# Where the variance of a batch norm is summed in a sparse graph-attention kernel: after the first attention, or beside it

## The chip, the cores and the metric

The kernel runs on one core of one Trainium2 chip, as one launch. The metric is the device time of that launch in microseconds, the median of a few runs. The core has five engines with an instruction queue each: TensorE (PE in the profile, with PEld for its weight loads), VectorE (DVE), ScalarE (ACT), GpSimd (POOL) and SyncE (SP, which here only issues DMAs). Each queue is worked off in order.

## The reference, cut to what matters

Four graph layers on 3327 nodes with 512 features each (8 heads of 64), over one sparse adjacency matrix. Each layer normalises its input, applies a layer function and adds the result to the input. Layer 0 is an attention followed by a batch norm over the nodes; layer 1 averages the neighbours' rows (GraphSAGE); layers 2 and 3 are attentions.

```
# layer 0, after the layer norm h of x
attn    = softmax(where(adj > 0, leaky_relu(s_dst[i] + s_src[j], 0.2), -9e15))
h_prime = einsum('ijh,jhd->ihd', attn, Wh).reshape(n, 512)
mean    = jnp.mean(h_prime, axis=0)
var     = jnp.var(h_prime, axis=0)
h_prime = gamma * (h_prime - mean) * jax.lax.rsqrt(var + 1e-5) + beta
x       = x + relu(h_prime)
# layer 1 starts from the layer norm of this x
```

Mean and variance run over all 3327 nodes, for each of the 512 features. So nothing of layer 1 can start before the last node of layer 0 is done.

## The kernel before, in words

The nodes are padded to 3328 and taken in 26 blocks of 128 (`NB`); a block is two groups of 64 destination nodes (`GB`). For each of the 52 groups, lists built at the start of the kernel hold the source nodes that the group needs, in chunks of 128; the chunk counts fall from 22 for the first group to 5 and 4 for the last (`CAPS`), 359 in all. A unit is up to three chunks of one group (`UNIT`), and there are 135 units.

The function `sparse` runs the layers one after the other. In `attend(layer, ...)` (from L1170) the loop over units does the following. `load(i + 1)` issues from POOL's queue one gather for each chunk of the next unit (L1165, an indirect DMA of 128 table rows into `rows`, which has six buffers); in layer 0 DVE also takes the mask bits out of the rows (`on`, L1252) and ACT turns them into `mask` (L1258). For the unit itself DVE makes `mx` (L1266, a maximum of two broadcasts, written to PSUM) and `wgt` (L1273, times the mask; three buffers), and PE multiplies `wgt` with the gathered rows into `facc` (L1287), where the last column of each head is the softmax's denominator. Between DVE's work and PE's matmuls of a unit, `later()` is called once. It lets every group that is through take one step of its `ending`: ACT copies the sums (L1215), DVE takes the reciprocal (L1219), ACT scales the eight heads into the result (L1225), and a finished block is reported. Then `later()` calls `tick()`.

In layer 0 the result goes to `y` (`bn_y`), which holds all 26 blocks in SBUF, a reported block is appended to `whole`, and `tick` advances a generator, `beside` (from L1339). That generator puts other work into the attention, one small step for each unit: 50 steps for the products of layer 1's weights (`fb_ps`, `fwx_ps`), then one step for each block of `y`, a matmul with a matrix of ones (L1374) that adds up the 128 nodes of the block in PSUM (`bmean_ps`). Every partition of the result holds the same sums. A float32 matmul appears as two in the profile.

PE, DVE and ACT are scheduled by hand inside `attend`: their instructions stay in the order in which the Python code issues them. The order in POOL's and SP's queues is left to the framework's scheduler.

After the attention come the mean (L1376), then the variance stage (pool `fbn`, L1398 to L1407): 13 rounds over two blocks each, in which DVE subtracts the mean into `bn_d` (two buffers), ACT squares it in place and PE adds the squares up in `var_ps`. The reciprocal root (`rsqrt`, L708 to L719) and the scaling of `gam`, `mean` and `bet` follow. Then `normed(c)` scales two blocks at a time, adds x, takes the layer norm for layer 1 and writes it to `h_dram`, while `own(c)` multiplies finished blocks with layer 1's weights. Layer 1 gathers its neighbours from `h_dram` (`z_rows`), so it starts when all 26 blocks have been written.

Of the kernel before, what the change touches and what calls it, by code (L numbers as in the profile page):

```python
# [23 lines left out]
F32 = mybir.dt.float32  # L24
# [7 lines left out]
AF = mybir.ActivationFunctionType  # L32
ALU = mybir.AluOpType
# [5 lines left out]
P = 128  # L39
H = 8  # L40
F = 64
D = H * F
# [8 lines left out]
GB = 64  # L51
CAPS = (22, 15, 13, 12, 11, 10, 9, 9, 9) + 4 * (8,) + 6 * (7,) + 11 * (6,) + 21 * (5,) + (4,)
HALF = 64
BATCH = 4
WB = 16
LNB = 5
ROW = H * (F + 1) + H
UNIT = 3
# [482 lines left out]
def constants(ctx, tc, N):  # L541
# [18 lines left out]

    c["pow"] = pw = const.tile([P, WB], F32, name="fpow")
    pi = const.tile([P, WB], I32, name="fpow_i")
    nc.gpsimd.iota(pi, pattern=[[-1, WB]], base=0, channel_multiplier=1)
    nc.vector.tensor_single_scalar(pi, pi, WB - 1, ALU.bitwise_and)
    for k in range(WB):
        nc.vector.memset(pw[:, k : k + 1], float(1 << k))
    nc.vector.scalar_tensor_tensor(pw, pi, 0.0, pw, ALU.is_equal, ALU.mult)
    c["bit"] = bit = const.tile([P, WB], U16, name="fbit")
    for k in range(WB):
# [4 lines left out]
class Projection:  # L574
# [13 lines left out]
    def stats(self, q):  # L588

        nc, pp, k = self.tc.nc, self.pool, q % LNB  # L590
        if q >= self.NB:
            return
        if k == 0:
            mv = pp.tile([P, LNB, nc.vector.BN_AGGR_DIM], F32, name="ln_mv", tag="ln_mv", bufs=2)
            self.mv, self.xs = mv, []
        xt = pp.tile([P, D], F32, name="ln_x", tag="ln_x", bufs=LNB + 4)
        nc.sync.dma_start(xt, self.xin[q * P : (q + 1) * P, :])
# [3 lines left out]
        self.xs.append(xt)  # L601
        if k == LNB - 1 or q == self.NB - 1:
            n = k + 1
# [4 lines left out]
    def norms(self):  # L608
        nc = self.tc.nc
        if self.step is not None:  # L610
            c0, n, mv, xs, step = self.step
            self.step = None
            r = step()
            ng = self.pool.tile([P, LNB, 1], F32, name="ln_ng", tag="ln_ng", bufs=2)
            if c0 + n == self.NB:
# [5 lines left out]
    def begin(self):  # L621
        self.step, self.have, self.turns, self.hT, self.wh, self.row, self.r = None, {}, 0, {}, {}, {}, {}
        for q in range(LNB):
            self.stats(q)
# [77 lines left out]
def rsqrt(nc, pool, cs, v, scale=1.0, bufs=3):  # L702


    n = v.shape[1]
    y = pool.tile([P, n], F32, name="rs_y", tag=f"rs_y{n}", bufs=bufs)
    g = pool.tile([P, n], F32, name="rs_g", tag=f"rs_g{n}", bufs=bufs)
    nc.scalar.activation(g, v, AF.Ln, scale=scale, bias=cs["eps"])  # L708
    nc.scalar.activation(y, g, AF.Exp, scale=-0.5)

    def step():
        h = pool.tile([P, n], F32, name="rs_h", tag=f"rs_h{n}", bufs=bufs)
        nc.vector.tensor_scalar(h, v, -0.5 * scale, -0.5 * EPS, ALU.mult, ALU.add)
        if n == 1:
            nc.vector.tensor_scalar(g, y, y, h, ALU.mult, ALU.mult)
        else:
            nc.vector.tensor_tensor(g, y, y, ALU.mult)
            nc.vector.tensor_tensor(g, g, h, ALU.mult)
        nc.vector.scalar_tensor_tensor(y, g, 1.5, y, ALU.add, ALU.mult)  # L719
        return y  # L720

    return step
# [17 lines left out]
class Following:  # L740
# [34 lines left out]
    mean = Projection.mean  # L775
# [361 lines left out]
def sparse(ctx: ExitStack, tc: tile.TileContext, t: dict, out: bass.AP, WA, ls, cs, idx, rdeg, first):  # L1137
# [5 lines left out]
    nc = tc.nc  # L1143
    N = out.shape[0]
    NP = t["x"].shape[0]
    NB = NP // P
# [3 lines left out]
    def used(c):  # L1150
        return min(P, N - c * P)
# [6 lines left out]
    ones = cs["ones"]  # L1158
# [171 lines left out]
    with ExitStack() as mx:  # L1330
        mid = mx.enter_context(tc.tile_pool(name="fmid", bufs=1))

        y = mid.tile([P, NB, D], F32, name="bn_y")
# [3 lines left out]
        whole = []  # L1337

        def beside(wp, wps):  # L1339

            nc.sync.dma_start(bias, t["L1_gnn_b_comb"].partition_broadcast(P))
            nc.sync.dma_start(gam, t["L0_gnn_gamma"].partition_broadcast(P))
            nc.sync.dma_start(bet, t["L0_gnn_beta"].partition_broadcast(P))
            for k, (wn, bn) in enumerate((("L1_WsT", "L1_gnn_b_self"), ("L1_WnT", "L1_gnn_b_nb"))):
                Wc = wp.tile([P, KC, D], F32, name="fWc", tag="fWc", bufs=1)
                nc.sync.dma_start(Wc, t["L1_gnn_W_comb"][k * D : (k + 1) * D, :].rearrange("(kc p) o -> p kc o", p=P))
                bcol = wp.tile([P, KC, 1], F32, name="b_col", tag="b_col", bufs=1)
                with nc.allow_non_contiguous_dma(reason="512 biases, once"):
                    nc.sync.dma_start(bcol[:, :, 0], t[bn].rearrange("(kc p) -> p kc", p=P))
                yield  # L1350
                b_bc = wp.tile([P, KC, P], F32, name="b_bc", tag="b_bc", bufs=1)
                nc.scalar.copy(b_bc, bcol.to_broadcast([P, KC, P]))
                ps = wps.tile([P, D], F32, name="fb_ps", tag="beside", bufs=1)
                for kc in range(KC):
                    nc.tensor.matmul(ps, b_bc[:, kc, :], Wc[:, kc, :], start=(kc == 0), stop=(kc == KC - 1))
                    yield
                nc.vector.tensor_tensor(bias, bias, ps, ALU.add)
                for fc in range(KC):
                    WT = wp.tile([P, KC, P], F32, name="fWT", tag="fWT", bufs=2)
                    nc.sync.dma_start(WT, t[wn][:, fc * P : (fc + 1) * P].rearrange("(kc p) o -> p kc o", p=P))  # L1360
                    yield
                    ps = wps.tile([P, D], F32, name="fwx_ps", tag="beside", bufs=1)
                    for kc in range(KC):
                        nc.tensor.matmul(ps, WT[:, kc, :], Wc[:, kc, :], start=(kc == 0), stop=(kc == KC - 1))
                        yield
                    w = wp.tile([P, D], F32, name="fwx", tag="fwx", bufs=1)
                    nc.scalar.copy(w, ps)
                    nc.sync.dma_start(wx_dram[k, fc, :, :], w)
            mean_ps = wps.tile([P, D], F32, name="bmean_ps", tag="beside", bufs=1)
            for c in range(NB):  # L1370
                while len(whole) <= c:
                    yield
                k = used(c)
                nc.tensor.matmul(mean_ps, ones[:k, :], y[:k, c, :], start=(c == 0), stop=(c == NB - 1))  # L1374
                yield
            nc.vector.tensor_scalar_mul(mean, mean_ps, 1.0 / N)  # L1376

        mean = mid.tile([P, D], F32, name="bn_mean")
        with tc.tile_pool(name="beside", bufs=1) as wp, tc.tile_pool(name="beside_ps", bufs=1, space=PSUM) as wps:
            bg = beside(wp, wps)  # L1380

            def done(c, hp, pool):
                yield
                whole.append(c)
                yield

            attend(0, *first, done, lambda: next(bg, None), y)
            for _ in bg:
                pass
# [5 lines left out]
        gps = mx.enter_context(tc.tile_pool(name="fsage_ps", bufs=2, space=PSUM))  # L1395
        two = [P, 2, D]
        with tc.tile_pool(name="fbn", bufs=1) as bp:
            var_ps = gps.tile([P, D], F32, name="var_ps", tag="n_ps")  # L1398
            for c in range(0, NB, 2):
                d = bp.tile(two, F32, name="bn_d", tag="bn_d", bufs=2)  # L1400
                nc.vector.tensor_tensor(d, y[:, c : c + 2, :], mean.unsqueeze(1).to_broadcast(two), ALU.subtract)
                nc.scalar.activation(d, d, AF.Square)
                for i in range(2):
                    k = used(c + i)
                    nc.tensor.matmul(var_ps, ones[:k, :], d[:k, i, :], start=(c + i == 0), stop=(c + i == NB - 1))
            var = bp.tile([P, D], F32, name="bn_var")
            nc.scalar.mul(var, var_ps, 1.0 / N)  # L1407
            nc.vector.tensor_tensor(gam, gam, rsqrt(nc, bp, cs, var, bufs=1)(), ALU.mult)
            nc.vector.tensor_tensor(mean, mean, gam, ALU.mult)
            nc.vector.tensor_tensor(bet, bet, mean, ALU.subtract)  # L1410
# [78 lines left out]
        for b in range(NB):  # L1489
            ps = list(zip_longest(*(list(ls.batches(b * PG + u, SUNIT)) for u in range(PG))))  # L1490
# [132 lines left out]
```

## Time and profile before

| what | us |
|---|---|
| median of 3 runs | 2559.43 (2559.01 to 2560.68) |
| the profiled execution | 2553.76 |
| its span | 2551.8 |

Where the span goes, and how busy the engines are in it, in us:

| stretch | stage | PE | DVE | ACT | POOL |
|---|---|---|---|---|---|
| 0 to 319 | adjacency, lists, projections of layer 0 | 204.7 | 215.2 | 134.5 | 19.0 |
| 319 to 807 | first attention | 328.2 | 452.8 | 175.1 | 341.3 |
| 807 to 842 | variance | 28.1 | 16.8 | 15.5 | 0.0 |
| 842 to 940 | batch norm, layer norm, own products | 77.1 | 82.8 | 36.9 | 7.6 |
| 940 to 1447 | layer 1, neighbours | 457.6 | 141.6 | 208.2 | 333.2 |
| 1447 to 2049 | second attention | 445.4 | 482.0 | 340.0 | 344.5 |
| 2049 to 2551 | third attention | 283.9 | 461.2 | 158.2 | 341.9 |

A line of the profile names the source line, the engine, the operation, what it writes and reads, and then either the start and duration (timeline) or the count, the busy time and the mean in ns (groups). In brackets or behind a bar stands how long the engine was idle just before, and what ended that idle time. A name after "<-" there is the releaser that the profile infers; "issue" means that it shows nothing that was waited for. Issuing an instruction is not counted as busy, so a queue can be full at less than full busy time.

### The profile page before, as it was taken

The numbers are of one execution on the slowest core, as the hardware profiler recorded it, in microseconds if no ns is written. First come the engines' busy times: TensorE is split into PE (matmuls) and PEld (weight loads), VectorE is DVE, ScalarE is ACT, GpSimd is POOL, SyncE is SP. The second block draws the span as 40 slices with busy tenths as digits, with TensorE's granted clock in tenths as the row PEclk, the third lists the DMA queues.
The fourth block names the chain that finished last, engine by engine and source line by source line (L and its number), as shares of the span: only waits on it lengthen the run. The fifth ranks groups of instructions, "written<-read, shape, count | busy, mean of one in ns | idle before, by whom it ended". The sixth has DMA issues, their size and how long they took to land.

```text
span 2551.8 us, 53690 instructions
## 1 busy us (share of the span) xinstructions
PE 1825.0 (72%) x21112; PEld 1161.8 (46%) x21112; DVE 1852.3 (73%) x2272; ACT 1068.3 (42%) x3810; POOL 1387.4 (54%) x1482
## 2 busy tenths in 40 slices
PE   3667756776677698889999657778878646566653
PEld 2444444454454342223333356656555435555543
DVE  7667579999997850222333499999877279999996
ACT  4553212333445332334455214667766601233444
POOL 1000176777772026777777277776554067777672
PEclk9767889988888899999999778897877787777787
DMA  8773198888783566788888478887665178888784
GB/s 326 288 263 123 43 296 276 280 281 260 241 253 95 191 217 198 234 247 260 254 267 255 125 223 242 235 240 232 199 200 177 39 215 232 236 238 243 232 238 123
DMA packets 189057, 562.57 MB, mean 220 GB/s; under 512 B 37764, under 2 KB 42304, under 8 KB 185470
## 3 DMA queue, kind: packets, MB, share of 16 engines
q0 software_dynamic: 115456, 404.86, 53.3%
q1 hardware_dynamic: 73342, 154.20, 17.0%
q8 instruction: 169, 2.77, 0.4%
q14 instruction: 90, 0.74, 0.1%
HBM read 499.26 MB, written 59.68 MB: 219 GB/s over the span
## 4 chain that ended last, share of the span: by engine, by line
PE 30%; DVE 24%; issue 13%; ACT 9%; DMA 8%; POOL 3%; DVEq 0%; SPq 0%; POOLq 0%; ACTq 0%
DVE mx L1266 12%; PE facc L1287 8%; DVE wgt L1273 8%; PE sage_acc L1522 4%; DMA z_rows<-h_dram,idx 4%; PE p_wh L866 4%; DMA rows<-table,idx 3%; PE n_ps L1471 3%; PE p_wh L808 3%; ACT fhp L1225 2%; POOL z_rows L1165 2%; PE s_ps L1445 2%; POOL rows L1165 1%; ACT bn_y L1225 1%; ACT v_row L870 1%
## 5 line engine op out<-in xcount | busy, mean ns | idle before, releaser
L1165 POOL DMA_INDIRECT rows<-table,idx x1077 | 1027.7, 954 | 580.0 <-issue 224.5
L1287 PE MATMUL facc<-rows,wgt 128*64 128x65 f32 x17232 | 722.5, 253 | 393.7 <-DVE wgt L1273 259.7
L1287 PEld LDWEIGHTS facc<-rows,wgt 128*64 128x64 f32 x17232 | 667.1, 165 | 518.2 <-DVE wgt L1273 310.5
L1266 DVE TENSOR_TENSOR mx<-r_bc,rows 128x1536 f32<-128x1536 f32 (+1 forms) x405 | 639.4, 1579 | 48.4 <-DMA fin_x<-fx 17.7
L1273 DVE TENSOR_TENSOR wgt<-mx,mask 128x1536 f32<-128x1536 f32 (+1 forms) x405 | 638.4, 1576 | 42.3 <-DVE mx L1266 1.0
L1165 POOL DMA_INDIRECT z_rows<-h_dram,idx x359 | 340.7, 949 | 273.7 <-ACT hT L1442 141.0
L1225 ACT ACTIVATE fhp<-sums,rd 64x64 f32<-64x64 f32 x832 | 219.9, 334 | 305.4 <-DVE rd L1219 302.0
L1522 PE MATMUL sage_acc<-z_rows,z_mask 128*64 128x512 f32 x718 | 209.8, 618 | 33.0 <-DMA z_rows<-h_dram,idx 32.6
L1258 ACT ACTIVATE mask<-on 128x192 uint8<-128x192 uint16 (+1 forms) x135 | 46.5, 345 | 325.3 <-DVE on L1252 321.8
L1086 POOL DMA_DIRECT2D list_b<-shift x12 | 6.0, 503 | 271.7 <-DVE shift L1040 271.5
L811 DVE TENSOR_TENSOR sd_pr<-p_wh,ab 128x1024 f32<-128x1024 f32 x26 | 31.8, 1225 | 141.4 <-PE p_wh L808 141.4
L1522 PEld LDWEIGHTS sage_acc<-z_rows,z_mask 128*64 128x64 f32 x718 | 52.2, 137 | 156.2 <-issue 77.6
L680 PE MATMUL wh_ps<-fWt,hT 128*128 128x512 f32 x208 | 123.3, 748 | 0.0
L866 PE MATMUL p_wh<-fWt,hT 128*128 128x512 f32 x208 | 117.2, 714 | 1.4 <-ACT s_col L860 1.4
L1225 ACT ACTIVATE bn_y<-sums,rd 64x64 f32<-64x64 f32 x416 | 109.5, 333 | 2.4 <-DVE rd L1219 0.5
L1503 ACT CAST z_mask<-mask 128x128 f32<-128x128 uint8 (+1 forms) x196 | 52.7, 284 | 118.7 <-PE sage_acc L1522 117.5
L1476 DVE TENSOR_TENSOR s_o<-n_ps,bn_y 128x512 f32<-128x512 f32 x26 | 17.9, 690 | 116.2 <-PE n_ps L1471 116.2
L1215 ACT COPY sums<-facc 128x260 f32<-128x260 f32 x156 | 56.6, 363 | 104.7 <-DMA rows<-table,idx 77.7
L1471 PE MATMUL n_ps<-fWx,aT 128*128 128x512 f32 x208 | 98.7, 608 | 0.0
L808 PE MATMUL p_wh<-fWt,hT 128*128 128x512 f32 x208 | 96.9, 610 | 2.0 <-DVE hT L699 1.9
L1445 PE MATMUL s_ps<-fWx,hT 128*128 128x512 f32 x208 | 93.5, 603 | 3.4 <-ACT hT L1442 3.4
L1198 PE MATMUL r_bc<-r_two,fones 2*128 2x512 f32 x156 | 89.1, 575 | 6.6 <-DMA r_two<-r_dram 3.6
(213 smaller groups left out, 2146.3 us busy)
## 6 DMA issues: line engine op xcount, KB each, us to landing
adj_i<-in_adj SPq DMA_DIRECT2D x26, 1664.0 KB
table<-v_row SPq DMA_DIRECT2D x78, 264.0 KB
rows<-table,idx POOLq DMA_INDIRECT x1077
fin_x<-fx SPq DMA_DIRECT2D x52, 256.0 KB
ln_x<-in_x SPq DMA_DIRECT2D x26, 256.0 KB
bn_x<-in_x SPq DMA_DIRECT2D x13, 512.0 KB
fx<-bn_x SPq DMA_DIRECT2D x13, 512.0 KB
fsage_x<-fx SPq DMA_DIRECT2D x26, 256.0 KB
```

Of the source, the lines that this page charges most:

```text
L680: nc.tensor.matmul(wh, hT[:, kc, :], self.Wt[:, kc, :], start=(kc == 0), stop=(kc == KC - 1))
L808: nc.tensor.matmul(wh, hT[:, kc, :], self.Wt[:, kc, :], start=(kc == 0), stop=(kc == KC - 1))
L866: nc.tensor.matmul(wh, hT[:, kc, :], self.Wt[:, kc, :], start=(kc == 0), stop=(kc == KC - 1))
L1165: nc.gpsimd.indirect_dma_start(out=dst, out_offset=None, in_=src[:, :], in_offset=bass.IndirectOffsetOnAxis(ap=idx[:, k : k + 1], axis=0))
L1198: nc.tensor.matmul(rb, ones[0:2, :].bitcast(F32R), rrs.pop(g).bitcast(F32R), start=True, stop=True)
L1225: nc.scalar.mul(hp[o0 : o0 + GB, h * F : (h + 1) * F], sm[mine, q, 0:F], rd[mine, q, :])
L1266: nc.vector.tensor_tensor(mx[:, :n], rbs[g].unsqueeze(1).to_broadcast(full), gt[:, :n, H * (F + 1) : ROW].unsqueeze(3).to_broadcast(full), ...
L1273: nc.vector.tensor_tensor(wt[:, :n], mx[:, :n], mk.unsqueeze(2).to_broadcast(full), ALU.mult)
L1287: nc.tensor.matmul(accs[g][v * GB : (v + 1) * GB, q * (F + 1) : (q + 1) * (F + 1)], wt[:, k, h, :], gt[:, k, h * (F + 1) : (h + 1) * (F + 1)],
L1445: nc.tensor.matmul(ps, hT[:, kc, :], Wx[:, 0, kc, :], start=(kc == 0), stop=(kc == KC - 1))
L1471: nc.tensor.matmul(ps, aT[:, kc, :], Wx[:, 1, kc, :], start=(kc == 0), stop=(kc == KC - 1))
L1522: nc.tensor.matmul(acc[u * GB : (u + 1) * GB, :], m, z, start=f, stop=l)
```

## The change

The variance is summed inside the first attention, by `beside`. The batch norm's sums are no longer taken about the mean, which is known only at the end, but about a `shift`, the mean of the first 8 blocks (`NSHIFT`). When these 8 blocks have been added up, ACT copies their mean to `shift`. From then on POOL subtracts `shift` from one block (`bn_d`, now four buffers), ACT squares it in place two or more steps later, and PE adds up the squares a step after that; one `tick` issues at most one of each, and one matmul in all. Both sums share one PSUM tile: the sums of `y` use 64 columns of ones and go to partitions 0 to 63 (`lo`), the squares use the other 64 and go to partitions 64 to 127 (`hi`). `taken` copies a half to both halves of its destination, so that all 128 partitions hold it. At the end the mean is put together from `shift` and the sum over the other 18 blocks, and the variance is the mean of the squares less the square of (mean - `shift`). The loop of the variance stage after the attention goes; the reciprocal root and what follows stay.

```diff
@@ -53,6 +53,7 @@
 HALF = 64
 BATCH = 4
 WB = 16
+NSHIFT = 8
 LNB = 5
 ROW = H * (F + 1) + H
 UNIT = 3
@@ -1366,15 +1367,51 @@
                     w = wp.tile([P, D], F32, name="fwx", tag="fwx", bufs=1)
                     nc.scalar.copy(w, ps)
                     nc.sync.dma_start(wx_dram[k, fc, :, :], w)
-            mean_ps = wps.tile([P, D], F32, name="bmean_ps", tag="beside", bufs=1)
-            for c in range(NB):
-                while len(whole) <= c:
-                    yield
-                k = used(c)
-                nc.tensor.matmul(mean_ps, ones[:k, :], y[:k, c, :], start=(c == 0), stop=(c == NB - 1))
+
+
+
+            ps = wps.tile([P, D], F32, name="bsum_ps", tag="beside", bufs=1)
+            lo, hi = slice(0, GB), slice(GB, P)
+
+            def taken(dst, src, scale):
+                for part in (lo, hi):
+                    nc.scalar.mul(dst[part, :], ps[src, :], scale)
+
+            made, squared = [], []
+            n = m = v = w = 0
+            while w < NB:
+                n += 1
+                if squared and squared[0][0] < n:
+                    _, d = squared.pop(0)
+                    k = used(w)
+                    nc.tensor.matmul(ps[hi, :], ones[:k, hi], d[:k, :], start=(w == 0), stop=(w == NB - 1))
+                    w += 1
+                elif m < len(whole):
+                    k = used(m)
+                    nc.tensor.matmul(ps[lo, :], ones[:k, lo], y[:k, m, :], start=(m in (0, NSHIFT)), stop=(m in (NSHIFT - 1, NB - 1)))
+                    m += 1
+                    if m == NSHIFT:
+                        taken(shift, lo, 1.0 / (NSHIFT * P))
+                if made and made[0][0] < n - 1:
+                    _, d = made.pop(0)
+                    nc.scalar.activation(d, d, AF.Square)
+                    squared.append((n, d))
+                if m >= NSHIFT and v < m and v < w + 4:
+                    d = wp.tile([P, D], F32, name="bn_d", tag="bn_d", bufs=4)
+                    nc.gpsimd.tensor_tensor(d, y[:, v, :], shift, ALU.subtract)
+                    made.append((n, d))
+                    v += 1
                 yield
-            nc.vector.tensor_scalar_mul(mean, mean_ps, 1.0 / N)
-
+            taken(mean, lo, 1.0 / N)
+            nc.vector.scalar_tensor_tensor(mean, shift, float(NSHIFT * P) / N, mean, ALU.mult, ALU.add)
+            nc.vector.tensor_tensor(shift, mean, shift, ALU.subtract)
+            nc.vector.tensor_tensor(shift, shift, shift, ALU.mult)
+            d = wp.tile([P, D], F32, name="bn_d", tag="bn_d", bufs=4)
+            taken(d, hi, 1.0 / N)
+            nc.vector.tensor_tensor(var, d, shift, ALU.subtract)
+
+        var = mid.tile([P, D], F32, name="bn_var")
+        shift = mid.tile([P, D], F32, name="bn_shift")
         mean = mid.tile([P, D], F32, name="bn_mean")
         with tc.tile_pool(name="beside", bufs=1) as wp, tc.tile_pool(name="beside_ps", bufs=1, space=PSUM) as wps:
             bg = beside(wp, wps)
@@ -1395,16 +1432,6 @@
         gps = mx.enter_context(tc.tile_pool(name="fsage_ps", bufs=2, space=PSUM))
         two = [P, 2, D]
         with tc.tile_pool(name="fbn", bufs=1) as bp:
-            var_ps = gps.tile([P, D], F32, name="var_ps", tag="n_ps")
-            for c in range(0, NB, 2):
-                d = bp.tile(two, F32, name="bn_d", tag="bn_d", bufs=2)
-                nc.vector.tensor_tensor(d, y[:, c : c + 2, :], mean.unsqueeze(1).to_broadcast(two), ALU.subtract)
-                nc.scalar.activation(d, d, AF.Square)
-                for i in range(2):
-                    k = used(c + i)
-                    nc.tensor.matmul(var_ps, ones[:k, :], d[:k, i, :], start=(c + i == 0), stop=(c + i == NB - 1))
-            var = bp.tile([P, D], F32, name="bn_var")
-            nc.scalar.mul(var, var_ps, 1.0 / N)
             nc.vector.tensor_tensor(gam, gam, rsqrt(nc, bp, cs, var, bufs=1)(), ALU.mult)
             nc.vector.tensor_tensor(mean, mean, gam, ALU.mult)
             nc.vector.tensor_tensor(bet, bet, mean, ALU.subtract)
```

## The prediction

> **What bounds the kernel now.** I read the table of busy time by stretch first, since the change takes work out of one stage and puts it into another.
>
> ```profile
> 319.00:560.00 241.00, 164.47 (x2881) 113.95 (x2881) 220.43 (x214) 64.83 (x219) 175.19 (x184) 0.90 0.89 285
> 560.00:807.00 247.00, 163.77 (x3050) 124.85 (x3047) 232.33 (x246) 110.22 (x398) 166.08 (x175) 0.85 0.76 234
> 807.00:842.00 35.00, 28.11 (x53) 9.72 (x52) 16.75 (x15) 15.48 (x20) 0.00 (x0) 0.90 0.00 0
> ```
>
> The columns are stretch, length, busy us of PE, PEld, DVE, ACT, POOL, then clock, DMA share and GB/s. The first two rows are the first attention: DVE is busy 94% of the second one and sets its pace. The third is the variance stage: 35 us in which no engine is full, POOL is empty and the DMA stands still. The groups of instructions in the second half of the attention show what POOL's 166 us hide:
>
> ```profile
> L1165 POOL DMA_INDIRECT rows<-table,idx x175 | 166.1, 949 | 63.9 <-issue 36.9 <-PE facc L1287 15.1 <-DVE mx L1266 5.6
> L1273 DVE TENSOR_TENSOR wgt<-mx,mask 128x1536 f32<-128x1536 f32 (+1 forms) x70 | 109.2, 1560 | 8.8 <-PE r_bc L1198 0.5
> L1266 DVE TENSOR_TENSOR mx<-r_bc,rows 128x1536 f32<-128x1536 f32 (+1 forms) x70 | 108.7, 1552 | 0.2 <-PE facc L1287 0.2
> ```
>
> A gather takes 0.95 us and the next starts 0.30 us after it, whoever is named as releaser. So a gather costs POOL's queue 1.25 us, and 175 of them fill 219 of 247 us. POOL is nearly as full as DVE. What is left is seen on POOL's own timeline at the end:
>
> ```profile
> 780.27 0.95 POOL L1165 DMA_INDIRECT rows<-table,idx  x1 [0.30 <-issue]
> 784.44 0.94 POOL L1165 DMA_INDIRECT rows<-table,idx  x1 [3.22 <-PE facc L1287]
> 788.18 0.94 POOL L1165 DMA_INDIRECT rows<-table,idx  x1 [0.30 <-issue]
> ```
>
> The 3.22 us is POOL running ahead until the six row buffers are full. From 564 us to the end I count six such waits: 3.74, 1.74, 1.30, 1.05, 0.41, 3.22. Less 0.30 each that is 9.7 us of free queue, 6.7 of it before the last.
>
> The variance stage on the timeline (start, duration, instruction):
>
> ```profile
> 806.25 1.13 PE L1374 MATMUL bmean_ps<-bn_y,fones 127*128 127x512 f32 x2 [3.07 <-ACT bn_y L1225]
> 807.42 0.69 DVE L1376 TENSOR_SCALAR bn_mean<-bmean_ps 128x512 f32<-128x512 f32 x1 [3.39 <-PE bmean_ps L1374]
> 810.57 5.90 PE L1405 MATMUL var_ps<-bn_d,fones 128*128 128x512 f32 x8 [3.19 <-ACT bn_d L1402]
> 841.77 0.72 ACT L708 ACTIVATE rs_g<-bn_var,feps 128x512 f32<-128x512 f32 x1
> ```
>
> The last y is written at 806.2; only at 841.77 does the logarithm of the reciprocal root start. These 35.6 us are one chain (DVE 1.22, ACT 1.06, PE four of 0.5 each, over two buffers) and nothing runs beside them.
>
> **What the Trainium skill says.** "GPSIMD Engine Reference", Elementwise — side-by-side cycle accounting: a two-input tensor_tensor on GpSimd takes about 2.6 cycles an element at 1.2 GHz, 4497 ns for 2048. The trace of before has no such instruction. "SBUF — State Buffer", Who interferes with whom: a DVE instruction with two SBUF inputs and a GpSimd instruction that reads SBUF lock each other out for a whole instruction. Of DVE's work here only `on` (L1252, 0.33 us, once a unit) has two SBUF inputs; mx and wgt each read one operand from PSUM. The trace of before cannot show the lock, as POOL only issues gathers there.
>
> **The change part by part.**
>
> *Removed from the path.* 13 rounds of subtract, square and four matmuls, with the first mean and the copy of var: all between 806.2 and 841.77.
>
> *What stands there instead*, from the last y (T), in the order that the built program has: POOL's subtract of the last block 1.2 (priced below), to T+1.3; its square 0.6 (half of the 1.06 of 128x1024, with some fixed part), T+2.0. PE meanwhile does the two sums still owed, 1.1 each behind the previous square, until T+2.8, then the last sum of squares, T+3.9. ACT copies the mean's two halves (bn_var's copy took 0.60) from T+2.9 to T+4.1, then the squares' two halves to T+5.3. DVE needs three operations of 0.69 after the mean, T+6.2, and the last makes var, T+6.9. The logarithm starts at T+7.0 where it was T+35.6. One z_mask cast (0.2) now stands between logarithm and exponential. **Gain 28.4 us.** What follows (scale, layer norm, projections, gathers) waits for that chain alone: the instructions and the bn_x loads keep their order and the kind of their waits, and the load of fWx was issued at 522. So all of it moves up.
>
> *PE in the attention*: 26 more pairs of matmuls, 64 columns instead of 128. That does not shorten them: sage_acc with 64 columns and 512 elements takes 593 ns, var_ps with 128 the same. 26 x 1.2 to 1.7 (mean bmean_ps 0.84 each here) is 31 to 44 us, into a PE busy 164 of 247. They stand ahead of the unit's facc matmuls; wgt has three buffers and rows six, so a lag of 1 to 2 us reaches nobody. Taken as 0; without that cover, the same 1 to 2 us per block on facc. *ACT*: 26 squares of 0.6, 16 us, into 110 of 247 busy. A square waits for a subtract emitted two units earlier; mask and sums queue behind it. POOL runs the subtract about 2.6 us after the gathers of the unit whose `on` the preceding mask needs, and that `on` waits 3.6 us for its rows: 0. *DVE*: nothing but the tail.
>
> *POOL in the attention*, the cost. The engine order of the built program puts four subtracts after the gathers of unit 69 of 135 (POOL is there at 563.8), five more by unit 76, and then one per block, behind the first gather of a unit four units later; 23 of 26 stand ahead of the last gathers, three behind. Their waits: the shift is copied at about 562, before POOL gets there; each y is about as old as the row buffer that POOL needs next anyway. So they cost queue time alone. Price: 512 x 2.6 / 1.2 = 1.11 us, a quarter of 4497 is 1.12. A fixed part of about 0.09 (POOL's memsets of 384 and 1664 elements took 0.41 and 1.48) and 0.1 of gap: **s = 1.3**. Floor 0.52, which those memsets give for 512 elements written and none read; ceiling 1.65, with another 0.30 gap. I take 1.3, since two reads must cost more than a fill.
>
> What does DVE see of it? Rows need time to land: where DVE waited for them in the second attention, mx began 3.0 us after the gather's end (1458.67 to 1461.66) for rows of 528 words; for the 632 here I estimate 3.6. Unit 131's gathers ended at 778.7 and its `on` began at 788.7: 10.0, of which 6.4 is spare. Ahead of it stand 22 subtracts, and POOL had 6.7 free: delay = 22 s - 6.7 - 6.4 = 22 x 1.3 - 13.1 = **15.5 us**. The last units give the same within 0.5. DVE begins to wait right after the first four (5.2 us of a lead of 8.1), and from there POOL sets the pace: a block of ten chunks takes it 12.5 + 1.3 = 13.8 us against DVE's 13.2. In that state the lock on `on` costs nothing, as DVE waits anyway; with DVE still pacing, it would be 23 x (1.2 / 3.4) x 0.6, about 5 us.
>
> **Sum.** -28.4 + 15.5 = -12.9. On the profiled execution 2553.8 - 12.9 = 2540.9 (span 2551.8 with 2 us around it). The median of the runs, 2559.4, lies 5.7 above that execution: **2546.5**.
>
> **The rivals.**
> *Hidden:* POOL's subtract is cheap (s near 0.6) and the gathers' lead covers it, 22 x 0.6 = 13.2 against 13.1 spare. Then the stage's 28 us are all gained: 2531. For it speaks DVE's 94%; against it that POOL's queue has 9.7 us free in 225. Chance 0.10.
> *A draw:* s between 1.65 and 2.11, delay 23 to 33, eats the gain to within 0.2%, which is about what a measurement of this kernel can tell from no change. Each subtract would have to bring a second gap or a switch between gather and arithmetic; no row shows one or excludes one. 2559. Chance 0.12.
> *Slower:* POOL's in-order queue stands at each subtract for y or for a free bn_d buffer, with gathers behind it, as the lead it used to run on is gone. The price is that wait per block, on top of 1.3; it decides from s = 1.88 on and counts from 2.11. At 2.4 the delay is 39.7: 2571. For it: y of a block is written within a microsecond of when POOL wants the next buffer (690.7 to 692.9, gather at 692.0). Against it: a late POOL finds y written. Chance 0.16.
> *Not doing what it says:* if all subtracts ran behind the last gather, the tail would hold 26 x 1.3 = 34 us and nothing be gained. The built order has 23 of them among the gathers, so I give it nothing.
>
> **The numbers.** Likeliest, 0.62: s from 1.1 to 1.65, delay 11 to 23, 2542 to 2554. Faster is this and the hidden case, 0.72; within 0.2% 0.12; slower 0.16. For eight in ten the range takes the likeliest case, half of the hidden and the draw: 2537 to 2564.
>
> **What would show it.** In the profile after: POOL subtracts of 1.1 to 1.3 us; from about 570 us on DVE's mx or `on` waiting for rows, some 15 us in all, and POOL without waits for facc; the attention ending near 822; the logarithm about 7 us after the last y. Wrong if DVE still shows no wait (hidden), if POOL shows long waits for ACT before subtracts (slower), or if the tail exceeds 10 us.

## The result, and the profile after

The changed kernel takes 2549.76 us (median of 6 runs, 2544.9 to 2552.2), the kernel before in the same comparison 2559.83 us (6 runs, 2554.76 to 2565.69). The ratio is 0.9961, with a 95% interval of 0.9945 to 0.9976: about 10 us faster, between 6 and 14. The profiled execution after took 2547.72 us, span 2545.8.

First the table of busy time by stretch, with the attention's second half and the stretch up to the logarithm (columns as before: PE, PEld, DVE, ACT, POOL, clock, DMA share, GB/s):

```profile
560.00:822.00 262.00, 185.28 (x3117) 131.31 (x3119) 251.75 (x249) 122.46 (x412) 201.11 (x203) 0.84 0.74 223
822.00:836.00 14.00, 5.30 (x37) 1.45 (x32) 3.08 (x7) 8.63 (x25) 2.02 (x2) 0.64 0.01 1
```

The 35 us stretch is gone, 14 us are left of it. The attention's second half has grown from 247 to 262 us, and DVE is busy for 252 of them, 19 more than before. Some 3 of these are units that fell ahead of 560 us before; the change gives DVE nothing to do there. The groups of that stretch say where:

```profile
L1166 POOL DMA_INDIRECT rows<-table,idx x178 | 170.9, 960 | 52.7 <-issue 37.3 <-PE facc L1288 7.6 <-DVE mx L1267 2.4
L1401 POOL TENSOR_TENSOR bn_d<-bn_y,bn_shift 128x512 f32<-128x512 f32 x25 | 31.8, 1279 | 8.5 <-ACT bn_y L1226 8.2
L1253 DVE TENSOR_TENSOR on<-rows,fbit 128x128 uint16<-128x128 uint16 (+1 forms) x71 | 38.8, 547 | 0.9 <-DMA rows<-table,idx 0.8
```

Two things are to be seen. POOL's subtract takes 1.28 us, and once it has begun to subtract POOL has no long waits left until the gathers are over (the 8.2 us lie behind the last one). And `on`, the extraction of the mask bits, takes 38.8 us instead of 22.7, with almost no wait ahead of it (0.9 us). Before:

```profile
L1252 DVE TENSOR_TENSOR on<-rows,fbit 128x192 uint16<-128x192 uint16 (+1 forms) x70 | 22.7, 325 | 0.0
```

One place on the timeline after, start and duration in the first two columns:

```profile
567.54 4.94 POOL L1401 TENSOR_TENSOR bn_d<-bn_y,bn_shift 128x512 f32<-128x512 f32 x4
570.08 2.55 DVE L1253 TENSOR_TENSOR on<-rows,fbit 128x128 uint16<-128x128 uint16 x1
572.56 1.22 DVE L1267 TENSOR_TENSOR mx<-r_bc,rows 128x1024 f32<-128x1024 f32 x1
```

`on` started while POOL was in its first four subtracts, and ended 0.15 us after the last of them. It is not waiting for rows: it is held inside the instruction, and the profile books that as busy time.

Since the first stage is a few us longer or shorter from one execution to the next (the first gather started at 319.4 before and at 323.5 after, which the change cannot touch), I measure the attention from the start of its first `on` to the end of its last `wgt`: 470.7 us before, 487.5 after, **16.8 longer**. From the last y to the logarithm it is 8.7 us instead of 35.6, **26.9 shorter**:

```profile
825.00 2.14 ACT L1226 ACTIVATE bn_y<-sums,rd 64x64 f32<-64x64 f32 x8 [0.24 <-DVE rd L1220]
827.21 1.26 POOL L1401 TENSOR_TENSOR bn_d<-bn_y,bn_shift 128x512 f32<-128x512 f32 x1 [4.45 <-ACT bn_y L1226]
829.60 1.92 PE L1387 MATMUL bsum_ps<-bn_d,fones 127*64 127x512 f32 x2
831.55 1.20 ACT L1378 ACTIVATE bn_mean<-bsum_ps 64x512 f32<-64x512 f32 x2 [2.42 <-PE bsum_ps L1387]
835.83 0.72 ACT L709 ACTIVATE rs_g<-bn_var,feps 128x512 f32<-128x512 f32 x1 [1.84 <-DVE bn_var L1411]
```

The sum, -10.1 us, is that of the medians. In the profiled pair the logarithm comes 5.9 us earlier and the end 6.0, the missing 4.1 being the late first gather. Nothing behind the logarithm moved against it.

### The profile page after: what moved, and what is told of

Read it like the earlier page. It is cut to its first block, busy times and chain, and to the rows that moved or that the text cites. A ratio compares the mean times of both kernels' runs of the same rounds, so it can differ in the third digit from the quotient of the medians.

```text
span 2545.8 us, 53721 instructions
## 1 busy us (share of the span) xinstructions
PE 1822.3 (72%) x21112; PEld 1161.3 (46%) x21112; DVE 1854.7 (73%) x2262; ACT 1072.6 (42%) x3828; POOL 1421.4 (56%) x1508
## 4 chain that ended last, share of the span: by engine, by line
PE 27%; DVE 24%; issue 13%; DMA 9%; ACT 8%; POOL 4%; DVEq 0%; SPq 0%; POOLq 0%; ACTq 0%
DVE mx L1267 12%; PE facc L1288 7%; DVE wgt L1274 7%; DMA z_rows<-h_dram,idx 5%; DMA rows<-table,idx 4%; PE sage_acc L1549 4%; PE p_wh L867 3%; PE p_wh L809 3%; PE n_ps L1498 3%; POOL rows L1166 2%; ACT fhp L1226 2%; POOL z_rows L1166 2%; DVE on L1253 2%; ACT v_row L871 1%; PE s_ps L1472 1%
## 5 line engine op out<-in xcount | busy, mean ns | idle before, releaser
L1288 PE MATMUL facc<-rows,wgt 128*64 128x65 f32 x17232 | 736.4, 254 | 363.3 <-DVE wgt L1274 243.2
L1288 PEld LDWEIGHTS facc<-rows,wgt 128*64 128x64 f32 x17232 | 683.2, 167 | 499.5 <-DVE wgt L1274 298.3
```

The lines of the kernel that those rows point to most:

```text
L1288: nc.tensor.matmul(accs[g][v * GB : (v + 1) * GB, q * (F + 1) : (q + 1) * (F + 1)], wt[:, k, h, :], gt[:, k, h * (F + 1) : (h + 1) * (F + 1)],
```

## The experiments

The theory after the result: POOL's queue time sets the delay of the attention (*queue*). The rival: POOL's time alone would be covered, and what costs is DVE held in `on` by subtracts that read SBUF (*lock*), since the 16.1 us by which `on` grew are nearly the whole delay. A third: the extra matmuls on PE and squares on ACT.

The expectations name times on the scale of the comparison above, where the kernel before took 2559.83 us. Beside experiments 1 to 4 it took 2553.91 us, beside 5 and 6 2555.65, so the ratio and the length of the attention are what to compare. Each length is that of one profiled execution; the three kernels without a delay (before, 1 and 3) agree within 0.3 us.

### 1. No subtract at all

```diff
-                    if m == NSHIFT:
-                        taken(shift, lo, 1.0 / (NSHIFT * P))
-                if made and made[0][0] < n - 1:
-                    _, d = made.pop(0)
-                    nc.scalar.activation(d, d, AF.Square)
+                if v < len(whole) and v < w + 4:
+                    d = wp.tile([P, D], F32, name="bn_d", tag="bn_d", bufs=4)
+                    nc.scalar.activation(d, y[:, v, :], AF.Square)
                     squared.append((n, d))
-                if m >= NSHIFT and v < m and v < w + 4:
-                    d = wp.tile([P, D], F32, name="bn_d", tag="bn_d", bufs=4)
-                    nc.gpsimd.tensor_tensor(d, y[:, v, :], shift, ALU.subtract)
-                    made.append((n, d))
                     v += 1
...
             taken(mean, lo, 1.0 / N)
-            nc.vector.scalar_tensor_tensor(mean, shift, float(NSHIFT * P) / N, mean, ALU.mult, ALU.add)
-            nc.vector.tensor_tensor(shift, mean, shift, ALU.subtract)
-            nc.vector.tensor_tensor(shift, shift, shift, ALU.mult)
+            nc.vector.tensor_tensor(shift, mean, mean, ALU.mult)
...
```

> No POOL work in the attention: ACT squares y itself, the sums of squares are taken about zero and the variance is E[y^2] - mean^2. PE's 26 extra matmul pairs and ACT's 26 squares stay. If the added time of the attention (16.8 us from the first mask bits to the last wgt) comes from POOL's subtracts, by its queue or by the lock on the mask bits, the attention is back at about 471 us, the tail loses the subtract (1.3 us) too, and the time is near 2531 us. If PE's or ACT's extra work is part of it, the attention stays some 3 to 10 us longer than before and the time is 2534 to 2541.

Measured: 2523.91 us against 2553.91 of the kernel before on the same chip, ratio 0.9885 (0.9869 to 0.9900). The attention is 470.4 us long, against 470.7 before; `on` is back at its old length; from the last y to the logarithm 5.9 us. The group of `on` in the attention's second half:

```profile
L1253 DVE TENSOR_TENSOR on<-rows,fbit 128x128 uint16<-128x128 uint16 (+1 forms) x69 | 22.4, 325 | 0.0
```

So the whole delay comes from the subtracts on POOL. The 26 pairs of matmuls and the 26 squares, which this kernel keeps, cost nothing, and the third theory is out. This kernel is also the fastest of the study, 30 us under the kernel before. Its price is in the numbers: it subtracts two quantities that are nearly equal where a feature's mean is large against its spread, which the shift was there to avoid. No run here tries such data.

### 2. POOL's time without reading

A fill writes to SBUF and reads nothing. Two fills take the subtract's place; ACT touches one column first, so that a fill waits for its block of y as the subtract did.

```diff
-                if made and made[0][0] < n - 1:
+                if made and made[0][0] < n - 3:
...
-                    nc.gpsimd.tensor_tensor(d, y[:, v, :], shift, ALU.subtract)
+                    e = wp.tile([P, 832], F32, name="bn_e", tag="bn_e", bufs=1)
+                    nc.scalar.copy(e[:, 0:1], y[:, v, 0:1])
+                    nc.gpsimd.memset(e, 0.5)
+                    nc.scalar.copy(d[:, 0:1], y[:, v, 0:1])
+                    nc.gpsimd.memset(d, 0.5)
```

> The subtract is replaced by two fills of 832 and 512 elements (about 1.3 us together, the duration of the subtract), which read nothing from SBUF; a touch of one column by ACT keeps the dependence on y, and the squares come two steps later. The summed values are constants, so the variance is left out. Queue theory: POOL's time alone sets the delay, so the attention is still 15 to 18 us longer than before, the mask bits fall back to 0.33 us each, DVE waits for rows instead, and the time is 2547 to 2552. Lock theory: what costs is DVE held in the mask bits (38.8 us against 22.5), so the attention falls to 471 to 475 us and the time to about 2533.

Measured: 2541.15 us, ratio 0.9947 (0.9933 to 0.9960); the attention 482.7 us long, 12.0 over before. The same group as above:

```profile
L1253 DVE TENSOR_TENSOR on<-rows,fbit 128x192 uint16<-128x192 uint16 (+1 forms) x70 | 22.9, 328 | 9.8 <-DMA rows<-table,idx 9.6
```

Now `on` is short and has waits for gathered rows ahead of it, 9.6 us in 16 places: the kind of wait that I had forecast for the change itself. Both simple theories fail. The queue costs 12 us without any lock; and the change costs nearly 5 us more than that. On POOL's timeline a block's fills lengthen the step from one gather to the next from 1.25 to 2.37 us, so 1.12 us of queue, and a subtract makes it 2.41, so 1.16. The long fill, then the changed kernel:

```profile
690.69 0.95 POOL L1166 DMA_INDIRECT rows<-table,idx  x1 [0.30 <-DVE rd L1220]
691.63 0.81 POOL L1403 MEMSET bn_e<- 128x832 f32 x1
692.36 0.54 POOL L1405 MEMSET bn_d<- 128x512 f32 x1
693.06 1.04 POOL L1166 DMA_INDIRECT rows<-table,idx  x1 [0.16 <-issue]
```

```profile
734.34 0.95 POOL L1166 DMA_INDIRECT rows<-table,idx  x1 [0.30 <-issue]
735.30 1.29 POOL L1401 TENSOR_TENSOR bn_d<-bn_y,bn_shift 128x512 f32<-128x512 f32 x1
736.75 0.96 POOL L1166 DMA_INDIRECT rows<-table,idx  x1 [0.16 <-DVE on L1253]
```

The difference of 0.04 is 0.9 us in 22 blocks. It leaves about 4 us of the 16.8 for the reading, that is, for the lock.

### 3. A short fill

```diff
-                    nc.gpsimd.tensor_tensor(d, y[:, v, :], shift, ALU.subtract)
+                    nc.scalar.copy(d[:, 0:1], y[:, v, 0:1])
+                    nc.gpsimd.memset(d, 0.5)
```

The squares come two steps later, as in the long fill (not shown).

> As the long fill, but one fill of 512 elements (about 0.5 us and a gap): 22 x 0.65 - 13.1 gives a delay of 1 us, at most 3. Both the queue and the lock theory expect an attention of 471 to 474 us and a time near 2533. If the number of interruptions of POOL counts rather than their length, or PE's and ACT's work, the attention stays 5 to 15 us longer.

Here too the values are constants, so the variance is left out. Measured: 2526.16 us, ratio 0.9897 (0.9882 to 0.9912); the attention 470.5 us long. A block costs POOL 0.40 us (from 1.25 to 1.65 between gathers), 22 of them 8.8 us, less than the 13.1 us of free queue and lead: no delay. The number of interruptions doesn't count; their length does, and only from a threshold on.

### 4. Each subtract twice

```diff
                     nc.gpsimd.tensor_tensor(d, y[:, v, :], shift, ALU.subtract)
+                    e = wp.tile([P, D], F32, name="bn_e", tag="bn_e", bufs=1)
+                    nc.gpsimd.tensor_tensor(e, y[:, v, :], shift, ALU.subtract)
```

> Each subtract is issued twice (the second into a scratch tile). Queue theory: s = 2.6, 22 x 2.6 - 13.1 = 44 us of delay instead of 15 to 17, the time about 2577, slower than before by 17. Lock theory: the held time doubles to 33 us, the time about 2566. If the delay had another cause, the time stays near 2550.

Measured: 2575.14 us, slower than the kernel before at a ratio of 1.0081 (1.0067 to 1.0094); the attention 515.5 us long, 44.8 over before. A block costs POOL 2.38 us.

```profile
L1253 DVE TENSOR_TENSOR on<-rows,fbit 128x128 uint16<-128x128 uint16 (+1 forms) x71 | 59.2, 833 | 8.5 <-DMA rows<-table,idx 8.5
```

```profile
569.11 7.43 DVE L1253 TENSOR_TENSOR on<-rows,fbit 128x128 uint16<-128x128 uint16 x1
```

`on` is held for 36 us in all, and there are 8.5 us of waits for rows besides. The first `on` beside subtracts lasted 7.43 us: POOL ran eight of them back to back, until 576.39, and DVE did not get in between two. The queue alone gives 22 x 2.38 - 13.1 = 39.3. The rest, 5.5, is little more than the changed kernel's (4.4), though twice as much is read.

### 5. The subtract on DVE

```diff
-                    nc.gpsimd.tensor_tensor(d, y[:, v, :], shift, ALU.subtract)
+                    nc.vector.tensor_tensor(d, y[:, v, :], shift, ALU.subtract)
```

> The subtract of each block is issued on DVE instead of POOL, at the same step. POOL's queue is as before, and there is no lock. DVE sets the pace without a gap, so 23 to 26 subtracts of 0.69 us and their 0.03 of spacing are paid in full: the attention is 16.5 to 18.5 us longer than before (after: 16.8), the mask bits take 0.33 us each, the tail is 0.6 us shorter than after's, and the time is within 3 us of the changed kernel. If DVE had slack that the trace does not show, the attention stays below 10 us over before and the time is 8 us or more under the changed kernel's.

Measured: 2544.6 us against 2555.65 before, ratio 0.9955 (0.9941 to 0.9968), which the interval cannot tell from the changed kernel's 0.9961. The attention is 487.3 us long, 16.6 over before; `on` has its old length.

```profile
L1253 DVE TENSOR_TENSOR on<-rows,fbit 128x128 uint16<-128x128 uint16 (+1 forms) x69 | 22.5, 326 | 0.0
L1401 DVE TENSOR_TENSOR bn_d<-bn_y,bn_shift 128x512 f32<-128x512 f32 x25 | 17.0, 681 | 3.1 <-ACT bn_shift L1378 3.1
```

The forecast came out, but not by its sum. Ahead of the last `wgt` stand 24 subtracts, and each adds 0.60 us to DVE's chain, as it starts a little before the instruction ahead of it has ended: 14.4 us. Another 3.1 us are a single wait: the first subtract stood on DVE until ACT had copied `shift`. So DVE has no slack, but a block there is somewhat cheaper than on POOL, where 16.8 us are 0.76 for each of 22. Whether the one wait could be avoided by a later first subtract was not tried.

### 6. Seven row buffers

```diff
-                gi = ap.tile([P, UNIT, width], I32, name="rows", tag="rows", bufs=6)
+                gi = ap.tile([P, UNIT, width], I32, name="rows", tag="rows", bufs=7 if layer == 0 else 6)
...
+            ring = wp.tile([P, KC, D], F32, name="bn_d", tag="fWc", bufs=1)
...
-                    d = wp.tile([P, D], F32, name="bn_d", tag="bn_d", bufs=4)
+                    d = ring[:, v % 4, :]
...
```

> The changed kernel with seven row buffers in the first attention instead of six (bn_d's four buffers lie in the space of the finished fWc). POOL can store one unit more of gathers, up to 3.75 us, ahead of the first subtract, where it waited for buffers for 8 us in the kernel before. Queue theory: the delay falls from 16.8 to about 13, the time by 3 to 4 us against the changed kernel. Lock theory (the lead is not what DVE is short of, it is held at the mask bits): the lead stays unused and the delay falls by 2 us or less.

Measured: 2540.36 us, ratio 0.9932 (0.9917 to 0.9947); the attention 482.4 us long, a delay of 11.7 instead of 16.8. POOL's last gather ended 483.6 us after its first, against 488.5. Of these 4.9 us a part is shorter gathers, for a reason given below (1.0 us over all of them, 1.8 over their second half); the other 3 to 4 us are the gathers stored ahead of the first subtract, of the 3.75 hoped for. The last unit's rows were issued 7.1 us ahead of use (after: 6.6), so the gain did not go into a longer lead; `on` became shorter in all by 3.9 us:

```profile
L1253 DVE TENSOR_TENSOR on<-rows,fbit 128x128 uint16<-128x128 uint16 (+1 forms) x71 | 34.9, 491 | 0.0
```

The lock theory's forecast, 2 us or less, fails: time given to POOL's queue reaches the end even while `on` is the place where it shows. Seven buffers without any subtract were not run.

### What they say together

s is the median step between gathers with a block's POOL work less the 1.25 us without, and "queue" is the prediction's own 22 s - 13.1 with the measured s.

| kernel | s | attention | delay | queue | rest |
|---|---|---|---|---|---|
| before | 0 | 470.7 | | | |
| short fill | 0.40 | 470.5 | -0.2 | 0 | 0 |
| long fill | 1.12 | 482.7 | 12.0 | 11.5 | 0.5 |
| after | 1.16 | 487.5 | 16.8 | 12.4 | 4.4 |
| twice | 2.38 | 515.5 | 44.8 | 39.3 | 5.5 |

With fills the queue's sum holds to half a microsecond. Where POOL reads SBUF, 4.4 and 5.5 us come on top; they are remainders of a sum, not durations that a profile shows. The Trainium skill says why ("SBUF — State Buffer", Who interferes with whom): the second operand of a DVE instruction with two SBUF inputs comes through a read interface that it shares with GpSimd, the sharing is an exclusive lock, and a GpSimd instruction that only writes does not contend. This case agrees on both sides: in the changed kernel `on`, with two inputs in SBUF, was held for up to 2.3 us beside subtracts, and it was not held at all beside fills, while mx and wgt, with one operand in PSUM, kept their 1.55 and 1.56 us.

The lock's 4 us show in two numbers. The last unit's lead (from the end of its gathers to its `on`) shrank from 8.9 us to 4.2 with the long fill, but only to 6.6 after: DVE, held at the subtracts, could not use up 2.4 us of lead. And POOL's last gather ended 488.5 us after its first, against 486.4 with the fills. Of those 2.1 us 0.9 are the dearer step. The rest are longer gathers, and the traces show which: those that begin while DVE is inside `on`. First the changed kernel, then experiment 5, where DVE's subtract takes the place of `on`:

```profile
725.36 0.35 DVE L1253 TENSOR_TENSOR on<-rows,fbit 128x192 uint16<-128x192 uint16 x1
725.40 1.13 POOL L1166 DMA_INDIRECT rows<-table,idx  x1 [0.30 <-issue]
```

```profile
565.87 0.67 DVE L1401 TENSOR_TENSOR bn_d<-bn_y,bn_shift 128x512 f32<-128x512 f32 x1
565.89 1.46 POOL L1166 DMA_INDIRECT rows<-table,idx  x1 [0.30 <-issue]
```

Over all eight profiles of this study, 160 gathers of the first attention last over 1.0 us (the first gather of each left out), and all 160 began inside `on` or inside DVE's subtract; of those begun at another time none is over 0.98. Over the second half of the gathers this costs 2.4 us in the changed kernel and 0.8 with the long fill, enough of a difference for the rest. So POOL's reads hold `on`, and DVE's two-input instructions hold gathers. What in a gather is held, no run shows.

## Why the prediction was right, point by point

The forecast was -12.9 us and 2546.5; measured were -10.1 us and 2549.76. The direction, the bound and the size held. Three terms did not. A cheaper subtract made the delay 22 x 0.14 = 3.1 us shorter than forecast, and the lock made it 4.4 longer; that these two nearly offset each other is luck. The removed stage gave 1.5 us less. Together that is the 2.8 us between -12.9 and -10.1.

*The removed stage*: 28.4 forecast, 26.9 measured. The logarithm starts 8.7 us after the last y, not 7.0. The step that failed is ACT's copy of the mean "from T+2.9" (T is the last y). It waited until T+4.4 for the last sum of squares, which goes to the other half of the same PSUM tile (its releaser in the chain above is L1387, not the sum of y at L1391), and that pair of matmuls took 1.92 us instead of 1.1, at a granted clock of 0.64 in this stretch.

*PE and ACT at nothing*: right; experiment 1 keeps both and the attention is as long as before.

*The price of a subtract*: mis-sized. 1.3 us forecast, 1.16 measured. The duration, 1.28, is a little over the forecast 1.2: the Trainium skill's price ("GPSIMD Engine Reference", Elementwise — side-by-side cycle accounting) for a quarter of the elements, 1.12 by estimate, and 0.09 of fixed part. But I added a gap, and the trace shows the reverse: arithmetic starts within 0.03 us of the gather's end, and the next gather 0.16 us after it instead of 0.30.

*Landing time*: 3.6 us estimated. In the long fill, at the 16 units that waited for their rows, it was 2.8 to 4.7, 3.5 on the mean.

*The lock at nothing, "as DVE waits anyway"*: this step was wrong. I had reckoned 5 us for it and then cancelled them, since a waiting DVE would absorb them. What happens is that the waiting moves: DVE reaches `on` with its rows there, meets the subtract that POOL issued behind an earlier gather, and is held. So the forecast of 15 us of waits for rows failed (0.8 us of them after), while their sum, as 16.1 us of longer `on`, was about right. The lock's own part is 4.4 us. That this is close to the 5 that I had struck out is chance, as the 5 was reckoned for DVE setting the pace. Nor was it so that the trace of before could not show the lock: 13 gathers there took 1.03 to 1.10 us instead of 0.95, and each began inside `on`.

*Queue*: right. With s = 2.38 the change is slower than before, as the prediction's line (slower beyond 2.11) has it; with 0.40 it is free, and the full stage is gained. *Break-even*: no run came near the forecast 1.88. With the measured 26.9 us of gain and some 5 of lock it would lie at (26.9 + 13.1 - 5) / 22 = 1.6, by estimate. The rival of waits for y in POOL's queue did not come: no subtract ahead of the last gather waited.

## What to carry to other kernels

Before work is moved to an engine "beside" a busy one, add up that engine's queue, not its busy share: POOL's 67% were 1.25 us per gather and a nearly full queue, and the work cost as much there (16.8 us) as on DVE itself (16.6, with one wait of 3.1 in it). Between such queues the slack is a store (buffers filled ahead) that is spent once; what exceeded it here was paid one for one and, where POOL read, a little more. The cheapest remedy is to have less of the work, as experiment 1 does. An instruction that grows in duration without a wait ahead of it may be held inside: look for what another engine was reading at that moment.

## What the runs showed of the hardware that was not expected

A POOL subtract of 128x512 costs less queue time than it lasts: 1.28 us long, 1.16 us of added time between two gathers. A lock shows as busy time: `on` lasted up to 2.55 us instead of 0.28, so that DVE was busy for 16 us more in a stage in which it had nothing more to do. Subtracts back to back kept DVE out for as long as they ran (7.43 us in experiment 4). And DVE held POOL too: a gather that began inside `on` lasted up to 1.13 us instead of 0.95, inside DVE's subtract up to 1.46.
